# A depthwise convolution re-cut from four 32-channel groups to eight 16-channel groups, with its pointwise on four bands and a fixed order of issue

## The chip, the cores and the metric

The kernel runs on one core of a Trainium2 chip. The metric is the device time of one execution in microseconds (us), the median of several runs. "The profile" and "the trace" are one execution taken by the hardware profiler. Engines: PE (matrix multiply; PEld is its weight load), DVE (vector), ACT (activation), POOL (GpSimd), and SP, whose queue issues nearly all DMAs here.

## The reference, cut to what matters

The input x is 16 images of 256 channels and 64 x 64 pixels, float32. Two layers follow each other:

```python
x = x + linear_attention(gn(x))   # layer 0: group norm, rms norm, q/k/v projection, softmax, context, output, rms norm
x = x + experts(gn(x))            # layer 1: the one that the change touches

def experts(x):                   # a router picks 2 of 4 experts for each image
    out = 0
    for i in the two chosen experts:
        h = depthwise_conv_3x3(x, dw_w[i]) + dw_b[i]     # every channel by itself, padding 1
        h = gelu(h)
        out += weight_i * (pw_w[i] @ h + pw_b[i])        # 256 x 256 over the channels
    return out
```

## The kernel before, in words

All 16 images go through one software pipeline. An image has a load-and-statistics stage, a projection stage, an attention stage and an expert stage, each on the time scale of 64 "slots"; stages of four successive images run side by side. A list of events, each a small function with a time in slots, is sorted by time and traced in that order; the scheduler of the language may then move instructions within its dependences. So image b + 2 is projected and image b + 1 attends while image b is in its expert stage. The projection makes four tiles `pq` for each of an image's eight token groups (`project`, L271) and ACT empties them (`evacuate`, L280 and L281). `po` (L340), `pss` (L257), `pc` (L287), `ptq` (L310) and `tr` (L366) are the other products of layer 0. Seven of the eight PSUM banks form one pool called `bank`.

The expert stage takes an image in four quarters of 16 rows (16 slots each). Its 256 channels are in two halves.

- Channels 128 to 255 go through DVE: `pad1` (L581 to L592) makes a padded copy on ACT, `start1` (L613) and eight `tap1` (L620) accumulate the nine taps for each of the two experts in `acc`, and `gelu1` (L627) finishes.
- Channels 0 to 127 go through PE. `pad0` (L546 to L563) normalizes a quarter into one buffer `pd0`, even and odd rows apart; there is a single `pd0`. `spread` (L569) copies it by DMA: for each of four groups of 32 channels, four DMAs put four row-shifted views on the four quarters of the partitions of a tile `xr`, so that a contraction over 128 partitions is one over 32 channels and 4 rows. That is 16 DMAs a quarter, each of 32 partitions by 528 floats. `conv0` (L598) makes 3 contractions of 512 columns for each group, one for each column offset, whose weights `taps` hold both experts and both row phases on the output partitions. `gelu0` (L605) writes the activated result back into `xr`.
- The pointwise for each half m of the output channels is `pointwise` parts 0 and 1 (L638, `acc`, 128 rows of weights, one bank for each row phase o) and parts 2 and 3 (L645, `xr`, where each row phase uses its own 64 partitions, a tile of 64 rows of the array). Its weights `psp` are spread once an image by 16 DMAs of 32 partitions (`spread_pw`, L529). `residual` (L653) adds the result to the ring of images in SBUF and `store` (L659) writes it out.

The loads are `load_a` (L201, `xa`), `load_b` (L204, `xb`) and `load_x1` (L80, `ring`), two or one DMA for each token group, all on SP's queue, as are `spread`, `spread_pw` and `store`. Every engine and every queue works in order.

The lines of `spread`, as an example of what one quarter issues:

```python
for r in range(NR):                      # NR = 4; called for g = 0..3
    nc.sync.dma_start(out=t[r * CH : (r + 1) * CH],
                      in_=pd0[g * CH : (g + 1) * CH, PH[r] : PH[r] + QF])
```

Of the kernel before, what the change touches and what calls it, by code (L numbers as in the profile page):

```python
# [16 lines left out]
P = 128  # L17
# [23 lines left out]
NR = 4  # L41
CH = P // NR
# [3 lines left out]
QF = QA * PW  # L46
# [3 lines left out]
LOGIT_CAP = 60.0  # L50


@with_exitstack
def pipelined_path(ctx, tc, wqkv, x, w_outT, b_out, g_out, router_wT, router_b, dw, dw_b, pwT, pw_b, out):
# [65 lines left out]

    id32 = const.tile([P, CH], FP, name="id32")
    nc.vector.tensor_tensor(id32, ident[:, 0:CH], ident[:, CH : 2 * CH], ALU.add)
    for r in range(2, NR):
        nc.vector.tensor_tensor(id32, id32, ident[:, r * CH : (r + 1) * CH], ALU.add)

    imask = const.tile([P, TOPK], FP, name="imask")
    nc.gpsimd.memset(imask, 0.0)
    for q in range(NR):
        nc.gpsimd.memset(imask[q * CH : (q + 1) * CH, q % 2 : q % 2 + 1], 1.0)
# [25 lines left out]
    tab = const.tile([P, CGR, NE, 2, 3], FP, name="tab")  # L155
    nc.gpsimd.memset(tab, 0.0)
    btab = const.tile([P, CGR, NE], FP, name="btab")
    for r in range(NR):
        rs = slice(r * CH, (r + 1) * CH)
        for o in range(2):  # L160
            if 0 <= r - o <= 2:
                for g in range(CGR):
                    nc.scalar.dma_start(
                        out=tab[rs, g, :, o, :],
                        in_=dw[g * CH : (g + 1) * CH, :, 3 * (r - o) : 3 * (r - o) + 3],
                    )
        nc.scalar.dma_start(
            out=btab[rs], in_=dw_b[0:P].rearrange("(g c) e u -> c g (e u)", c=CH)
        )


    pd0 = const.tile([P, 2 * (QF + PW)], FP, name="pd0")
    nc.gpsimd.memset(pd0, 0.0)
    PH = [QF + PW, 0, QF + 2 * PW, PW]
# [312 lines left out]
    def pick_rows(b, i):  # L487

        oh = live["oh", b]
        wv = live["wv", b] if i else new(small, [P, CGR, 3, 2, TOPK], "wv", b, bufs=1)  # L490
        wt = new(small, [P, CGR, 6, NE], "wt", b, i, bufs=1)
        nc.vector.tensor_tensor(
            wt, tab.rearrange("p g e o x -> p g (o x) e"),
            oh[:, i].unsqueeze(1).unsqueeze(1).to_broadcast([P, CGR, 6, NE]), ALU.mult,
        )
        nc.vector.tensor_reduce(
            wv[:, :, :, :, i].rearrange("p g x o -> p g o x"),
            wt.rearrange("p g (o x) e -> p g o x e", o=2), AX.X, ALU.add,
        )
# [12 lines left out]
    def build_taps(b, g):  # L512

        wv = live["wv", b]
        t = new(work, [P, 3 * P], f"taps{g}", b, bufs=1)
        nc.gpsimd.tensor_tensor(
            t.rearrange("p (n c) -> p n c", c=CH),
            wv[:, g].rearrange("p x o i -> p (x o i)").unsqueeze(2).to_broadcast([P, 12, CH]),
            id32.unsqueeze(1).to_broadcast([P, 12, CH]), ALU.mult,
        )  # L520

    def spread_pw(b):

        t, src = new(work, [P, CGR, C], "psp", b, bufs=1), live.pop(("pw0", b))
        for o in range(2):
            for i in range(TOPK):
                q = 2 * o + i
                for g in range(CGR):
                    nc.sync.dma_start(  # L529
                        out=t[q * CH : (q + 1) * CH, g], in_=src[g * CH : (g + 1) * CH, i]  # L530
                    )
# [8 lines left out]
    def pad0(b, j, s):  # L540

        sck, bik = scale1(b, 0)
        if s == 0:
            top = pd0[:, QF + PW + 1 : QF + PW + 1 + W]
            if j == 0:
                nc.gpsimd.memset(top, 0.0)  # L546
            else:
                last = QF + PW + QF
                nc.gpsimd.tensor_copy(top, pd0[:, last + 1 : last + 1 + W])
        base = 0 if s == 0 else QF + 2 * PW  # L550
        nc.scalar.activation(
            pd0[:, base : base + QF].rearrange("p (a w) -> p a w", w=PW)[:, :, 1 : W + 1],
            x1c(b, j)[:, 0].rearrange("p (a s w) -> p a s w", s=2, w=W)[:, :, s],
            AF.Identity, bias=bik, scale=sck,
        )
        if s == 1:
            low = pd0[:, QF + 1 : QF + 1 + W]
            if j < NQ - 1:
                nc.scalar.activation(
                    low, x1c(b, j + 1)[:, 0, 0:W], AF.Identity, bias=bik, scale=sck  # L560
                )
            else:
                nc.gpsimd.memset(low, 0.0)  # L563

    def spread(b, j, g):

        t = new(work, [P, QF], "xr", b, j, g, bufs=6)
        for r in range(NR):
            nc.sync.dma_start(  # L569
                out=t[r * CH : (r + 1) * CH],  # L570
                in_=pd0[g * CH : (g + 1) * CH, PH[r] : PH[r] + QF],
            )
# [21 lines left out]
    def conv0(b, j, g):  # L594
        po = live["dw", b, j, g] = bank("dw", b, j, g)
        rows3 = live["xr", b, j, g].rearrange("p (a w) -> p a w", w=PW)
        for d in range(3):
            nc.tensor.matmul(  # L598
                po, live[f"taps{g}", b][:, d * P : (d + 1) * P], rows3[:, :, d : d + W],
                start=(d == 0), stop=(d == 2),  # L600
            )

    def gelu0(b, j, g):

        nc.scalar.activation(  # L605
            live["xr", b, j, g][:, 0:GT], live.pop(("dw", b, j, g)), AF.Gelu,
            bias=live["bv", b][:, g : g + 1],
        )
# [20 lines left out]
    def pointwise(b, j, m, part):  # L629

        ms = slice(m * P, (m + 1) * P)
        if part == 0:
            live["ppw", b, j, m] = [bank("pw", b, j, m, o) for o in range(2)]
        po = live["ppw", b, j, m]
        if part < TOPK:
            h = live["acc", b, j, part].rearrange("p (a o) w -> p a o w", o=2)
            for o in range(2):
                nc.tensor.matmul(  # L638
                    po[o], live["pw1", b][:, part, ms], h[:, :, o], start=(part == 0), stop=False
                )  # L640
            return
        for g in range(2 * part - 4, 2 * part - 2):
            for o in range(2):
                half = slice(o * P // 2, (o + 1) * P // 2)
                nc.tensor.matmul(  # L645
                    po[o], live["psp", b][half, g, ms], live["xr", b, j, g][half, 0:GT],
# [3 lines left out]
    def residual(b, j, m, o):  # L650
        po = live["ppw", b, j, m][o]
        xo = x1c(b, j)[:, m].rearrange("p (a o w) -> p a o w", o=2, w=W)[:, :, o]
        nc.vector.scalar_tensor_tensor(  # L653
            xo, po.rearrange("p (a w) -> p a w", w=W),
# [8 lines left out]

    events = []

    def at(t, f, *args):
        events.append((t, len(events), f, args))

    for b in range(NB):
        T = PERIOD * b  # L670
        for g in range(NG):
            t = T + SLOT * g
            if b:
                at(t - 5, load_a, b, g)
            at(t + 3, stats, b, g)
        for i, f in enumerate((gn0_mean, gn0_dev, gn0_scale, gn0_bias)):
            at(T + 60 + i, f, b)
        for g in range(NG):
            t = T + 65 + SLOT * g
            if b:  # L680
                at(t - 6, load_b, b, g)
            at(t, norm, b, g, 0)
            at(t + 1, norm, b, g, 1)
            at(t + 2, add_squares, b, g)
            at(t + 3, sum_squares, b, g)
            at(t + 3.5, token_scale, b, g)
            for c in range(CG):
                at(t + 5 + c // 2, project, b, g, c)
                at(t + 6 + c // 2 - 0.5, evacuate, b, g, c)
            at(t + 8, context, b, g)  # L690
            at(t + 8, q_sum, b, g)
            at(t + 9, q_norm, b, g)
            at(t + 10, q_turn, b, g)
            at(t + 11, q_keep, b, g)
        at(T + 130, mix_a, b)
        at(T + 131, mix_b, b)
        at(T + 132, mix_c, b)
        for g in range(NG):
            t = T + 136 + SLOT * g
            if b:  # L700
                at(t + 2, load_x1, b, g)
            for hf in range(2):
                at(t + hf, attend, b, g, hf)
                at(t + hf + 0.9, out_squares, b, g, hf)
                at(t + hf + 2, out_scale, b, g, hf)
                at(t + hf + 3, out_norm, b, g, hf)
            for k in range(KH):
                at(t + 5, out_turn, b, g, k)
                at(t + 6, out_add, b, g, k)
                at(t + 7 + k, square_sums, b, g, k)  # L710
        R = T + 201
        at(R, gn1_sums, b)
        at(R + 1, gn1_scale, b)
        at(R + 2, router, b)
        at(R + 3, choose, b)
        at(R + 5, pick_taps, b)
        E = T + 217
        at(E - 9, weigh, b)
        at(E - 8, pick_bias, b)
        at(E - 6, pick_row_bias, b)  # L720
        for i in range(TOPK):
            at(E - 7 + i, pick_rows, b, i)
            for e in range(NE):
                at(E - 5 + 2 * i + e / 2, pick_pw, b, 0, i, e)
                at(E + 11 + 2 * i + e / 2, pick_pw, b, 1, i, e)
        for g in range(CGR):
            at(E + 1 + g, build_taps, b, g)
        at(E + 11, spread_pw, b)
        for j in range(NQ):
            t = E + 16 * j  # L730
            at(t - 3, pad1, b, j)
            for i in range(TOPK):
                at(t - 1 + 7 * i, start1, b, j, i)
# [643 lines left out]
```

## Time and profile before

| | |
|---|---|
| median of 3 runs | 3365.88 us (3356.1 to 3371.1) |
| the profiled execution | 3348.74 us, of which the span of the program is 3346.9 us |
| mean granted PE clock | 0.963 |
| PE busy | 3082.2 us (92%) |
| DVE, ACT, POOL busy | 2366.2, 2222.3, 909.2 us |
| DMAs of `xr`, `psp` | 1024 and 256 |
| ACT table loads | 308, of 1283 ns each |

Shares of busy time are means over the span. Groups give the count, the union of the busy time, the mean of one instruction, and the idle time before it with what ended it. A matmul of float32 stands as two records, each with its own weight load, and the recorded length of one is longer than the distance to the next, because they are pipelined; the distances are what add up. DMA-issuing instructions are not counted as busy; the queue's own timeline shows them.

### The profile page before, as it was taken

How to read it: one execution, taken by the hardware profiler on the slowest of the kernel's cores; microseconds unless marked ns; L12 is line 12 of the kernel's file. 1: busy time of each engine (PE TensorE's matmuls, PEld its weight loads, DVE VectorE, ACT ScalarE, POOL GpSimd, SP SyncE). 2: the span in 40 equal slices, each digit the busy share in tenths (PEclk: the TensorE clock that was granted, in tenths of full speed). 3: DMA queues.
4: the chain of work that ended last, by engine and by line, in shares of the span. 5: the costliest groups of instructions: out<-in, count | busy, mean ns of one | idle time of the engine just before them, and what ended most of it. 6: DMA issues, size and time to landing. Idle time of an engine off the chain costs nothing. (4 is left out here: it accounts for less than half of the span.)

```text
span 3346.9 us, 38011 instructions
## 1 busy us (share of the span) xinstructions
PE 3082.2 (92%) x11476; PEld 1716.7 (51%) x11476; DVE 2366.2 (71%) x4076; ACT 2222.3 (66%) x4308; POOL 909.2 (27%) x943
## 2 busy tenths in 40 slices
PE   4888999999999999999999999999999999999988
PEld 2565555554555555555555555555555555554433
DVE  4447677777677676786776776766786776678886
ACT  2577667676776766767676676767777776775432
POOL 2234222232222322223232222323223232222210
PEclk9798999999999999999999999999999999999999
DMA  7422333334334342342434333332232233222322
GB/s 226 153 81 84 117 92 108 120 89 123 96 92 127 102 127 81 104 127 88 129 92 126 91 108 108 92 99 73 88 101 85 87 95 97 75 77 79 106 70 71
DMA packets 189380, 342.06 MB, mean 102 GB/s; under 512 B 36848, under 2 KB 45552, under 8 KB 189168
## 3 DMA queue, kind: packets, MB, share of 16 engines
q1 hardware_dynamic: 182560, 338.16, 33.1%
q10 hardware_dynamic: 6608, 1.39, 0.2%
q8 instruction: 95, 1.56, 0.2%
q14 instruction: 117, 0.96, 0.1%
HBM read 194.72 MB, written 67.11 MB: 78 GB/s over the span
## 5 line engine op out<-in xcount | busy, mean ns | idle before, releaser
L620 DVE SCALAR_TENSOR_TENSOR acc<-pd,ds,acc 128x1024 f32<-128x1024 f32 x1024 | 1326.0, 1320 | 13.8 <-ACT acc L613 6.7
L598 PE MATMUL dw<-xr,taps 128*128 128x512 f32 x1536 | 740.7, 622 | 0.8 <-DVE ring L653 0.8
L271 PE MATMUL pq<-wqkv_n,xg 128*128 128x384 f32 x2048 | 715.0, 503 | 2.2 <-DVE ring L375 2.2
L271 PEld LDWEIGHTS pq<-wqkv_n,xg 128*128 128x128 f32 x2048 | 394.8, 196 | 317.6 <-issue 69.2
L645 PE MATMUL pw<-xr,psp 64*128 64x512 f32 x2048 | 527.2, 633 | 0.0
L638 PE MATMUL pw<-acc,pw 128*128 128x512 f32 x1024 | 487.6, 600 | 20.0 <-ACT acc L627 20.0
L598 PEld LDWEIGHTS dw<-xr,taps 128*128 128x128 f32 x1536 | 289.8, 198 | 284.2 <-issue 275.3
L302 POOL TENSOR_TENSOR e<-e,qs 128x512 f32<-128x512 f32 x128 | 144.7, 1131 | 1007.3 <-DVE qs L298 666.5
L382 ACT ACTIVATE sqj<-ring,nm 128x512 f32<-128x512 f32 x256 | 184.4, 720 | 333.7 <-DVE ring L375 326.6
L186 POOL TENSOR_TENSOR s<-s,mhalf 128x2 f32<-128x2 f32 x256 | 245.0, 957 | 343.0 <-DVE s L185 342.4
L359 DVE TENSOR_TENSOR ob<-po,s 128x512 f32<-128x512 f32 x256 | 176.9, 691 | 198.9 <-POOL s L186 198.9
L247 ACT ACTIVATE sq<-xb,bi,sc 128x512 f32<-128x512 f32 x240 | 183.9, 809 | 176.2 <-PE pss L257 176.0
L280 ACT ACTIVATE e<-pq,r 128x256 f32<-128x256 f32 x512 | 245.3, 479 | 71.0 <-PE pq L271 69.1
L645 PEld LDWEIGHTS pw<-xr,psp 64*128 64x128 f32 x2048 | 182.4, 192 | 208.3 <-issue 205.7
L638 PEld LDWEIGHTS pw<-acc,pw 128*128 128x128 f32 x1024 | 187.6, 193 | 196.9 <-issue 150.0
L297 DVE TENSOR_REDUCE qs<-e 128x16 f32<-128x512 f32 x128 | 87.6, 684 | 262.0 <-ACT e L280 261.4
L340 PE MATMUL po<-mw,qt 128*128 128x256 f32 x1024 | 263.6, 382 | 0.7 <-DVE ring L375 0.3
L340 PEld LDWEIGHTS po<-mw,qt 128*128 128x128 f32 x1024 | 192.2, 190 | 103.4 <-issue 33.5
L375 DVE SCALAR_TENSOR_TENSOR ring<-tr,gout,ring 128x512 f32<-128x512 f32 x256 | 181.6, 745 | 81.4 <-PE tr L366 81.1
L287 PE MATMUL pc<-vr,e 128*128 128x129 f32 x1024 | 156.1, 285 | 86.5 <-ACT vr L281 82.9
L653 DVE SCALAR_TENSOR_TENSOR ring<-pw,bs,ring 128x512 f32<-128x512 f32 x256 | 184.3, 744 | 63.7 <-PE pw L645 63.7
L251 POOL TENSOR_TENSOR sq<-sq 128x512 f32<-128x512 f32 x128 | 203.0, 1586 | 94.2 <-issue 59.4
(138 smaller groups left out, 3754.3 us busy)
## 6 DMA issues: line engine op xcount, KB each, us to landing
xr<-pd SPq DMA_DIRECT2D x1024, 66.0 KB, 2.0
ring<-in_x SPq DMA_DIRECT2D x256, 256.0 KB, 3.2
out<-ring SPq DMA_DIRECT2D x128, 512.0 KB, 2.8
xa<-in_x SPq DMA_DIRECT2D x120, 512.0 KB, 4.2
xb<-in_x SPq DMA_DIRECT2D x120, 512.0 KB, 4.0
psp<-pw SPq DMA_DIRECT2D x256, 32.0 KB, 1.9
pw<-in_pwT ACTq DMA_DIRECT2D x1, 1024.0 KB, 8.4
wqkv_n<-in_w_qkvT SPq DMA_DIRECT2D x1, 384.0 KB, 3.2
```

The source lines that it names most:

```text
L186: nc.gpsimd.tensor_tensor(out_t, out_t, mhalf[:, :n], ALU.pow)
L247: nc.scalar.activation(live["sq", b, g][:, k], xb[:, k], AF.Square, bias=bi, scale=sc)
L251: nc.gpsimd.tensor_tensor(sq[:, 0], sq[:, 0], sq[:, 1], ALU.add)
L271: nc.tensor.matmul(pq, xg[:, k, c * P : (c + 1) * P], wqkv[:, k], start=(k == 0), stop=(k == KH - 1),)
L280: nc.scalar.activation(live["e", b, g][:, c], pq[:, : 2 * HID], AF.Exp, scale=r)
L340: nc.tensor.matmul(po[:, c], qt[:, n * P : (n + 1) * P], live["mw", b], start=True, stop=True)
L382: nc.scalar.activation(junk, x1(b, g)[:, k], AF.Square, bias=live["nm", b][:, k : k + 1], accum_out=live["sm", b][:, 1, k, g : g + 1],)
L598: nc.tensor.matmul(po, live[f"taps{g}", b][:, d * P : (d + 1) * P], rows3[:, :, d : d + W], start=(d == 0), stop=(d == 2),)
L620: nc.vector.scalar_tensor_tensor(acc, pd1[j % 2][:, t // 3 : t // 3 + QR, t % 3 : t % 3 + W], live["ds", b][:, i, t : t + 1], acc, ALU.mul ...
L638: nc.tensor.matmul(po[o], live["pw1", b][:, part, ms], h[:, :, o], start=(part == 0), stop=False)
L645: nc.tensor.matmul(po[o], live["psp", b][half, g, ms], live["xr", b, j, g][half, 0:GT], start=False, stop=(g == CGR - 1),)
L653: nc.vector.scalar_tensor_tensor(xo, po.rearrange("p (a w) -> p a w", w=W), live["bs", b][:, m : m + 1], xo, ALU.add, ALU.add,)
```

## The change

1. Depthwise on PE: channel groups go from four of 32 to eight of 16. Rows and columns are both split by parity (`pd0` now holds four phases), and each of 8 pieces of 16 partitions of `xr` holds one view: 4 row shifts by 2 column phases. A group needs 2 contractions of 256 columns; two groups share a bank. `spread` issues 8 DMAs of 16 partitions by 264 floats for each group, 64 a quarter. `xr` has 12 buffers in place of 6.
2. The output partitions of a contraction are 4 pixel phases by 2 experts by 16 channels, so the pointwise from `xr` runs on four bands of 32 partitions, one bank for each pixel phase; the pointwise from `acc` reads pixel phases with a stride of two. Four banks are held until both halves m have been added. `residual` runs on 256 elements, eight times a quarter. `psp` takes 64 DMAs of 16 partitions an image.
3. `pad0` writes each row phase by two ACTIVATEs, one for each column phase. `gelu0` runs on 256 elements, eight times a quarter.
4. The tables for the taps are made in the setup by DVE in place of 24 small DMAs.
5. The timetable: all times come from a table `WAIT`, and the events are traced under `tc.manual_schedule()`, so that instructions stay in the order of the list.

```diff
-NR = 4
-CH = P // NR
+NPC = 8
+CH = P // NPC
...
-    pd0 = const.tile([P, 2 * (QF + PW)], FP, name="pd0")
+    pd0 = const.tile([P, 2, 2, QA + 1, PC], FP, name="pd0")
...
+        for v in range(NPC):
+            for g in range(CGR):
+                nc.sync.dma_start(
+                    out=t[v * CH : (v + 1) * CH, g], in_=src[g * CH : (g + 1) * CH, v % 2]
+                )
...
+        def put(rows, slot, n, src):
+            for t in range(2):
+                nc.scalar.activation(
+                    pd0[:, rows, t, slot : slot + n, t : t + W // 2],
+                    src.rearrange("p a (c t) -> p a c t", t=2)[:, :, :, t],
+                    AF.Identity, bias=bik, scale=sck,
+                )
...
-        t = new(work, [P, QF], "xr", b, j, g, bufs=6)
-        for r in range(NR):
+        t = new(work, [P, QA * PC], "xr", b, j, g, bufs=12)
+        for v in range(NPC):
+            a = v // 4
             nc.sync.dma_start(
-                out=t[r * CH : (r + 1) * CH],
-                in_=pd0[g * CH : (g + 1) * CH, PH[r] : PH[r] + QF],
+                out=t[v * CH : (v + 1) * CH],
+                in_=pd0[g * CH : (g + 1) * CH, v // 2 % 2, v % 2, a : a + QA].rearrange(
+                    "c a w -> c (a w)"
+                ),
             )
...
-        for d in range(3):
+        for d in range(2):
             nc.tensor.matmul(
-                po, live[f"taps{g}", b][:, d * P : (d + 1) * P], rows3[:, :, d : d + W],
-                start=(d == 0), stop=(d == 2),
+                po, live[f"taps{g}", b][:, d * P : (d + 1) * P], rows3[:, :, d : d + W // 2],
+                start=(d == 0), stop=(d == 1),
             )
...
-        for g in range(2 * part - 4, 2 * part - 2):
-            for o in range(2):
-                half = slice(o * P // 2, (o + 1) * P // 2)
+        for g in range(4 * part - 8, 4 * part - 4):
+            for q in range(4):
+                band = slice(q * P // 4, (q + 1) * P // 4)
                 nc.tensor.matmul(
-                    po[o], live["psp", b][half, g, ms], live["xr", b, j, g][half, 0:GT],
+                    po[q], live["psp", b][band, g, ms], live["xr", b, j, g][band, 0 : GT // 2],
                     start=False, stop=(g == CGR - 1),
                 )
...
+            at(t + WAIT["pad0"], pad0, b, j, 0)
+            at(t + WAIT["pad0"] + 0.01, pad0, b, j, 1)
+            for g in range(CGR):
+                at(t + WAIT["pad0"] + 0.02 + WAIT["spread"] + WAIT["spread_g"] * g, spread, b, j, g)
+            for g in range(0, CGR, 2):
+                u = t + WAIT[f"conv{g // 2}"]
+                at(u, conv0, b, j, g)
+                at(u, conv0, b, j, g + 1)
+                at(u + WAIT["gelu0"], gelu0, b, j, g)
+                at(u + WAIT["gelu0"], gelu0, b, j, g + 1)
+            t += 2 * SLOT - 0.5 + WAIT["gelu1_1"] + WAIT["pointwise"]
...
     events.sort(key=lambda e: e[:2])
-    for _, _, f, args in events:
-        f(*args)
+    with tc.manual_schedule():
+        for _, _, f, args in events:
+            f(*args)
```

With t the slot at which a quarter begins, the new table puts `pad0` at t + 3, `spread` from t + 3.52 to t + 5.27, the four pairs of `conv0` at 11.37 (groups 2, 3), 12.36 (4, 5), 13.2 (0, 1) and 16.9 (6, 7), and the parts of `pointwise` from t + 16.95 on, one slot apart. `spread_pw` stands at 10.84 of an image's first quarter.

## The prediction

> **What bounds the kernel now.** First the page's engine sums and a steady stretch of the stage table (columns: busy time with the number of instructions for PE, PEld, DVE, ACT, POOL, then PE's granted clock, DMA share, GB/s).
>
> ```profile
> PE 3082.2 (92%) x11476; PEld 1716.7 (51%) x11476; DVE 2366.2 (71%) x4076; ACT 2222.3 (66%) x4308; POOL 909.2 (27%) x943
> 1000.00:2600.00 1600.00, 1516.13 (x5714) 842.66 (x5713) 1152.26 (x1993) 1130.92 (x2160) 447.78 (x453) 0.97 0.34 102
> ```
>
> PE works 95% of steady time, DVE 72%, ACT 71%: PE bounds it. SP is in neither line. So second the timelines of SP's queue at two successive images' psp bursts, and its two kinds of DMA (duration min/median/max in ns, first and last start):
>
> ```profile
> 2147.60 10.03 SPq L529 DMA_DIRECT2D psp<-pw  x16
> 2158.04 0.34 SPq L659 DMA_DIRECT2D out<-ring  x1
> ...
> 2345.12 10.04 SPq L529 DMA_DIRECT2D psp<-pw  x16
> 2355.26 0.53 SPq L659 DMA_DIRECT2D out<-ring  x1
> 2355.88 1.82 SPq L569 DMA_DIRECT2D xr<-pd  x3
> ```
> ```profile
> L569 SPq DMA_DIRECT2D xr<-pd x1024: 507/582/1722, 287.1 to 3316.8; - x171
> L529 SPq DMA_DIRECT2D psp<-pw x256: 512/589/1907, 283.2 to 3244.8; - x128
> ```
>
> An image takes 197.5 us here, 202 in the median over the run; a quarter is 50.5. Sixteen SBUF-to-SBUF DMAs take SP 10.03 us: 0.63 each with the gap, and the same for rows of 1 KB (psp) and of 2.1 KB (xr). An issue costs SP time whatever it carries. Today an image has 80 of them and 40 loads and stores of about 0.45: 68 of 202 us. Third, the waits on the single pd0, which show that the next pad stands behind the last spread:
>
> ```profile
> POOL pd L549 <- DMA xr<-pd: 181.3, 46, 17.5
> ACT pd L551 <- DMA xr<-pd: 56.0, 18, 6.8
> ```
>
> Fourth PE's distances, and its weight loads (columns start, length, what):
>
> ```profile
> 1649.86 5.32 PE L271 MATMUL pq<-wqkv_n,xg 128*128 128x384 f32 x16
> 1655.02 1.03 PE L340 MATMUL po<-mw,qt 128*128 128x256 f32 x4
> 1655.89 2.74 PE L598 MATMUL dw<-xr,taps 128*128 128x512 f32 x6
> ```
> ```profile
> 1613.44 0.30 PEld L217 LDWEIGHTS pg<-mv,gmean 128*128 128x128 f32 x2
> 1613.76 0.30 PEld L645 LDWEIGHTS pw<-xr,psp 64*128 64x128 f32 x4
> ```
>
> From start to start: eight pq matmuls of 384 columns 5.16 us (0.645 each), two po of 256 columns 0.87 (0.43 each). One of 512 takes 0.86. In the second fence two loads of 128 rows take 0.30 us and four loads of 64 rows also 0.30: loads of different row bands run side by side.
>
> **The change, part by part.** *PE.* A quarter's conv0 goes from 12 x 0.86 = 10.3 us to 16 x 0.43 = 6.9: 3.4 less, 14 an image. The pointwise from acc stays 6.9 (16 of 256 columns for 8 of 512). From xr, four bands share the array where two do: 64 matmuls x 0.43 / 4 = 6.9, as now. [...] The load row above (four in the time of two) speaks against queueing, so I count 6.9.
>
> *DVE* gets 8 residuals of 256 (0.49, the pw row of L485) for 4 of 512 (0.74): +0.9 us a quarter, and the picks of the tap tables, 256 elements for 96, under 2 an image: 38 of 50 us become 39. *ACT* gets 8 gelus at about 0.48 (the e row, 256 elements) for 4 at 0.68, and 3 more pad instructions (0.45 to 0.6): +2.7 a quarter, while the program's order needs 110 table loads for 308: -198 x 1.283 = -254 us in all, -4.0 a quarter. *POOL* +2 us an image. The setup loses some ACT DMAs; at most 8 us, before the first statistics are ready. All this is off the path while PE or SP sets it. Four of seven banks held may make PE wait on ACT's evacuations: 0 to 1 us a group; it disappears under what follows. So do the longer lists of waits (PE's separate wait instructions go from 996 to 2313 in the program, 17 to 50 ns each, at most 4 us an image) and what the fixed order shifts elsewhere.
>
> *SP.* The program issues 4096 + 1024 such DMAs for 1024 + 256. Rows of 16 partitions aren't in the trace. Bounds for one: below, 0.43, the distance of an xa load (378 ns, 128 partitions, one side in HBM); above, 0.63, since psp and xr agree although one carries twice the other. The shortest xr issue of 1024 is 0.507. I take 0.63: same path (SBUF to SBUF), same 16-fold division, and size has no effect. So one spread is 64 x 0.63 = 40.3 us, psp another 40.3, and SP needs 5 x 40.3 + 40 x 0.48 = 221 us an image, over the 202 it has. SP becomes the bound even if it never waits.
>
> *It waits, too.* There is one pd0, and under the fixed order the next pad on ACT stands behind the evacuations of a projection, which stands on PE behind the pair of conv0 (slot 16.9) that needs the last spread. Queued behind that one DMA wait on PE: that conv0 (16.9), pointwise parts 0 and 1 (16.95, 17.95), the projection (18.1); on ACT gelu0, four evacuations (18.8), pad0 (19.0); on SP the next spread. From the last issue's end: landing 2.0 - 0.6 = 1.4; conv0 pair 4 x 0.43 = 1.7; pointwise 8 x 0.43 = 3.4; projection 8 x 0.645 = 5.2; last evacuation 0.9 (0.479 + 0.373); pad0 4 at about 0.6 + 2 at 0.43 (from 0.804 at 512 and 0.453 at 64 elements), overlapping, 2.8. Sum 15.4 us. SP has 10 loads and stores for it, 4.8 us, and sits idle for the rest. The other pairs of conv0 are not later: from 75% of the burst to its end PE has two pairs, ptq and tr, about 6 of 10 us. Nor are the 12 buffers of xr: groups 4 to 7 wait for the last pointwise of the quarter before, some 27 us after the handoff starts; the spread reaches them after 15.4 + 20.
>
> So a quarter is 40.3 + 15.4 = 55.7 us, and the first, where psp is issued during the handoff, 40.3 + 4.8 + 40.3 = 85.4. An image: 85.4 + 3 x 55.7 = 252.5. The last two images have no projection behind them: handoff 6.9, fewer loads, 225. PE's 44 us a quarter, DVE's 39 and ACT's 34 fit inside.
>
> Sum: first spread at 287 (as now), 14 x 252.5 = 3535, 2 x 225 = 450, and after the last spread 24 (landing 1.4, conv0 1.7, pointwise 14, residual and store 7): 4296, and 2 outside the span. The profiled execution lies 0.5% under the median of the runs; I say **4300**.
>
> An unknown above: idle waits of PE may lower its clock. The slices at the start, where PE is busy 205 of 287 us, have 0.89 granted: 12% of the 10.3 us of PE in a handoff, 48 times, +60 us. [...]
>
> **The rivals.** *Faster: the small issue is cheap.* If 16 partitions cost c, an image's loop is 320c + 3 x 15.4 + 4.8; it is under 202 for c below 0.47. At 0.43 it is 189, and PE with 202 - 14 = 188 is level: 16 x 12 us less, about 3170. For it: an xa load costs 0.43. Against: no xr or psp issue took under 0.507. [...]
>
> *Slower, but the loop is shorter.* If the pad did not wait for the projection, or c is the 0.57 seen behind an idle moment, then 3800 (issue alone: 287 + 14 x 221 + 2 x 205 + 24) to 3980 (64c = 36.5 with the whole handoff).
>
> *Slower by PE.* Cheap issues, but the bands' loads queue at the 0.11 us that the loads of pss stand apart (seven in 0.86): 128 x 0.11 = 14.1 for 6.9 us a quarter, less 3.4 gained: 54 a quarter, about 3570.
>
> That the contraction isn't halved as said is excluded: the program has 16 conv0 matmuls of 256 columns a quarter.
>
> **How the numbers follow.** The full loop (4000 to 4480) 0.66; the shorter loop (3600 to 4000) 0.18; cheap issue, faster, 0.11; PE's loads 0.03; no change 0.02, where c happens to fall at 0.47. No change is within 0.5%, about what a measurement of this kernel tells apart. Slower 0.87, faster 0.11. The range reaches down into the shorter loop, leaving out the cheap issue and the rest: 3700 to 4480.
>
> **What would show it.** Right: xr issues near 0.58 us, 64 in a row over 40 us; psp bursts 250 us apart; PE's share down to about 66%, its longest waits those of dw on the DMA of xr; pads waiting on evacuations or on xr's DMAs; SP's longest wait that of L586 on ACT. Wrong: xr issues under 0.47; or SP late but pads early (the loop is shorter); or loads of psp one after another at 0.11.

## The result, and the profile after

The changed kernel takes 4518.3 us (median of four runs, 4511.96 to 4521.58) where the kernel before takes 3364.5 on the same chip: a ratio of 1.343, with a 95% interval of 1.3395 to 1.3463. The forecast was 4300 with a range up to 4480. The direction and the mechanism held; the time lies 218 us above the forecast and 38 above the range. The profiled execution took 4521.58 us, its span 4519.8.

The engine sums and the same steady stretch of the stage table as before (busy time with instructions for PE, PEld, DVE, ACT, POOL, then PE's granted clock, DMA share, GB/s):

```profile
PE 3275.1 (72%) x19156; PEld 2423.3 (54%) x19156; DVE 2427.6 (54%) x4368; ACT 2092.9 (46%) x4542; POOL 1093.3 (24%) x1002
1000.00:2600.00 1600.00, 1202.51 (x7124) 891.33 (x7123) 889.75 (x1598) 782.06 (x1686) 414.40 (x360) 0.85 0.27 84
```

No engine of this line is full any more: PE fell from 95% to 75% of steady time, and its granted clock from 0.97 to 0.85. The chain that ended last, by engine, has SP's queue on top:

```profile
SPq 42%; PE 37%; DMA 9%; issue 4%; ACT 2%; DVE 2%; POOL 1%; ACTq 0%; DVEq 0%; POOLq 0%
```

The two kinds of DMA, as groups of one tile (duration min/median/max in ns, first and last start), and SP's timeline over a part of an image:

```profile
L586 SPq DMA_DIRECT2D xr<-pd x4096: 507/587/1921, 273.0 to 4491.4; - x196
L545 SPq DMA_DIRECT2D psp<-pw x1024: 507/587/1646, 316.0 to 4353.8; - x171
```
```profile
2102.05 41.89 SPq L586 DMA_DIRECT2D xr<-pd  x64
2143.99 0.58 SPq L223 DMA_DIRECT2D xb<-in_x  x1
2144.61 0.94 SPq L94 DMA_DIRECT2D ring<-in_x  x2
...
2153.93 1.56 SPq L94 DMA_DIRECT2D ring<-in_x  x2
...
2160.66 42.16 SPq L586 DMA_DIRECT2D xr<-pd  x64
...
2205.51 43.81 SPq L545 DMA_DIRECT2D psp<-pw  x64
...
2253.83 41.38 SPq L586 DMA_DIRECT2D xr<-pd  x64
```

An issue of 16 partitions by 264 floats has the median of 587 ns that one of 32 partitions by 528 floats had before (582), so a spread of four times the pieces takes SP 41.9 us here. Between two spreads lie 16.7 us here (2143.94 to 2160.66), 17.3 in the mean over the middle of the run; loads of `xb` and `ring` are issued at the start of that gap, behind the burst. Now the same gap on PE, in order of time (in brackets the idle time before, and what ended it):

```profile
2145.43 1.40 PE L619 MATMUL dw<-xr,taps 128*128 128x256 f32 x4 [3.96 <-DMA xr<-pd]
2146.62 2.76 PE L660 MATMUL pw<-acc,pw 128*128 128x256 f32 x6
2149.96 0.72 PE L660 MATMUL pw<-acc,pw 128*128 128x256 f32 x2 [0.57 <-DVE ring L394]
2151.06 2.08 PE L660 MATMUL pw<-acc,pw 128*128 128x256 f32 x8 [0.39 <-ACT acc L648]
2152.98 5.32 PE L290 MATMUL pq<-wqkv_n,xg 128*128 128x384 f32 x16
...
2159.88 2.01 PE L668 MATMUL pw<-xr,psp 32*128 32x256 f32 x32
2161.82 1.13 PE L359 MATMUL po<-mw,qt 128*128 128x256 f32 x4
```

The order is the predicted one: the pair of `conv0` (its first half has run at 2140.37, so that two of its four matmuls are left), pointwise parts 0 and 1, the projection. But conv0 and pointwise stand there for 7.55 us (2145.43 to 2152.98), where 5.1 was counted: PE waits for DVE and for ACT in between, and ACT and DVE wait for the two loads that SP issued right behind the burst, at 2143.99 and 2144.61:

```profile
2148.07 0.81 ACT L265 ACTIVATE xg<-xb,bi,sc 128x512 f32<-128x512 f32 x1 [7.50 <-DMA xb<-in_x]
...
2149.96 1.05 ACT L648 ACTIVATE acc<-acc 128x1024 f32<-128x1024 f32 x1
```
```profile
2149.15 0.75 DVE L394 SCALAR_TENSOR_TENSOR ring<-tr,gout,ring 128x512 f32<-128x512 f32 x1 [11.38 <-DMA ring<-in_x]
```

PE's clock falls in such gaps too. Two rows of the stage table, each from PE's last wait in the pointwise to the projection, for the same eight records of the pointwise; the first is the gap above, the second the one that begins at 2353.4:

```profile
2151.06:2152.98 1.92, 1.92 (x9) 1.61 (x9) 1.05 (x4) 1.92 (x4) 0.43 (x1) 1.00 1.06 431
2360.41:2363.37 2.96, 2.96 (x8) 2.33 (x9) 2.58 (x5) 2.96 (x7) 1.47 (x3) 0.62 1.02 413
```

Of 33 gaps in the middle of the run, those without psp, 18 last 16.5 to 16.7 us. The other 15 last 17.7 to 20.0, with a clock of 0.50 to 0.68 behind PE's last wait.

In the fence of PE's gap the last rows answer a rival: 32 records of the four-band pointwise, which are 16 matmuls, take 1.94 us (2159.88 to 2161.82), and 16 x 0.43 / 4 is 1.72. Four bands do run side by side.

Who was late is in the waits of the engines and of SP's queue (total us, times, longest):

```profile
DVE ring L394 <- DMA ring<-in_x: 646.2, 63, 21.4
PE dw L619 <- DMA xr<-pd: 625.1, 204, 8.9
ACT xg L265 <- DMA xb<-in_x: 336.2, 54, 8.5
```
```profile
SPq L94 <- DMA out<-ring: 307.5, 100, 7.4
SPq L586 <- ACT pd L562: 291.3, 78, 14.8
```

PE's longest wait is for `xr`, as forecast, and SP's wait for the pad on ACT is there, though as SP's second longest. The waits of ACT for `xb` (336.2 us) and of DVE for the ring's loads (646.2 us) were not. SP's 5746 DMAs start in this trace in the order in which the kernel lists them, and so do the instructions of ACT and DVE in the pipeline: both engines stand before a load that SP issued only behind the burst.

### The profile page after: what moved, and what is told of

Its sections match the earlier page's. It is cut to its first block, busy times and chain, and to the rows that moved or that the text cites. A ratio compares the mean times of both kernels' runs of the same rounds, so it can differ in the third digit from the quotient of the medians.

```text
span 4519.8 us, 60126 instructions
## 1 busy us (share of the span) xinstructions
PE 3275.1 (72%) x19156; PEld 2423.3 (54%) x19156; DVE 2427.6 (54%) x4368; ACT 2092.9 (46%) x4542; POOL 1093.3 (24%) x1002
## 4 chain that ended last, share of the span: by engine, by line
SPq 42%; PE 37%; DMA 9%; issue 4%; ACT 2%; DVE 2%; POOL 1%; ACTq 0%; DVEq 0%; POOLq 0%
SPq L586 30%; SPq L545 11%; PE pq L290 9%; PE pw L668 8%; PE pw L660 8%; PE dw L619 4%; PE po L359 3%; DMA out<-ring 3%; DMA xb<-in_x 2%; DMA xr<-pd 2%; DMA ring<-in_x 1%; PE pc L306 1%; PE pss L276 1%; PE tr L385 1%; ACT xg L265 1%
## 5 line engine op out<-in xcount | busy, mean ns | idle before, releaser
L619 PE MATMUL dw<-xr,taps 128*128 128x256 f32 x2048 | 728.4, 507 | 676.9 <-DMA xr<-pd 625.1
L619 PEld LDWEIGHTS dw<-xr,taps 128*128 128x128 f32 x2048 | 487.1, 254 | 850.5 <-issue 574.4
L668 PE MATMUL pw<-xr,psp 32*128 32x256 f32 x8192 | 601.4, 410 | 384.9 <-DMA psp<-pw 384.9
L668 PEld LDWEIGHTS pw<-xr,psp 32*128 32x128 f32 x8192 | 441.0, 197 | 490.3 <-DMA psp<-pw 416.2
L660 PE MATMUL pw<-acc,pw 128*128 128x256 f32 x2048 | 589.5, 438 | 72.8 <-DVE ring L394 32.3
L394 DVE SCALAR_TENSOR_TENSOR ring<-tr,gout,ring 128x512 f32<-128x512 f32 x256 | 190.9, 747 | 782.2 <-DMA ring<-in_x 646.2
L660 PEld LDWEIGHTS pw<-acc,pw 128*128 128x128 f32 x2048 | 426.6, 215 | 209.6 <-DVE ring L394 47.2
L627 ACT ACTIVATE xr<-dw,bv 128x256 f32<-128x256 f32 x512 | 213.1, 467 | 665.9 <-PE dw L619 506.8
L367 ACT ACTIVATE junk<-po 128x256 f32<-128x256 f32 x512 | 195.2, 381 | 651.7 <-PE po L359 642.4
L205 POOL TENSOR_TENSOR r<-r,mhalf 128x4 f32<-128x4 f32 x128 | 222.5, 1738 | 882.5 <-DVE r L204 788.7
L265 ACT ACTIVATE xg<-xb,bi,sc 128x512 f32<-128x512 f32 x240 | 193.9, 808 | 339.0 <-DMA xb<-in_x 336.2
L204 DVE TENSOR_SCALAR s<-ss 128x2 f32<-128x2 f32 x256 | 58.1, 227 | 493.4 <-ACT junk L367 493.3
L677 DVE SCALAR_TENSOR_TENSOR ring<-pw,bs,ring 128x256 f32<-128x256 f32 x512 | 222.7, 475 | 46.0 <-PE pw L668 46.0
## 6 DMA issues: line engine op xcount, KB each, us to landing
xr<-pd SPq DMA_DIRECT2D x4096, 16.5 KB, 1.8
```

Source lines behind the costliest of these rows:

```text
L205: nc.gpsimd.tensor_tensor(out_t, out_t, mhalf[:, :n], ALU.pow)
L265: nc.scalar.activation(live["xg", b, g][:, k], xb[:, k], AF.Identity, bias=bi, scale=sc)
L619: nc.tensor.matmul(po, live[f"taps{g}", b][:, d * P : (d + 1) * P], rows3[:, :, d : d + W // 2], start=(d == 0), stop=(d == 1),)
L660: nc.tensor.matmul(po[q], live["pw1", b][:, part, ms], h[:, :, q // 2, :, q % 2], start=(part == 0), stop=False,)
L668: nc.tensor.matmul(po[q], live["psp", b][band, g, ms], live["xr", b, j, g][band, 0 : GT // 2], start=False, stop=(g == CGR - 1),)
L677: nc.vector.scalar_tensor_tensor(xo, po.rearrange("p (a c) -> p a c", c=W // 2), live["bs", b][:, m : m + 1], xo, ALU.add, ALU.add,)
```

## The experiments

Two questions: is it SP's issues and the handoff through the single `pd0` at all (theory A), or PE (B) or the fixed order (C)? And what made each quarter about 4 us longer than forecast? All but the spread through HBM are single runs.

**The pad 1.25 slots earlier.**

```diff
-    "pad0": 3, "spread": 0.5,
+    "pad0": 1.75, "spread": 0.5,
```

> The changed kernel with pad0 at slot 1.75 of its quarter in place of 3, so that on ACT it stands behind gelu0 of the last pair of conv0 but ahead of the four evacuations of the projection. Theory A (SP's queue sets the time: 64 issues of about 0.65 us a quarter, then a handoff of 17 us through the single pd0): the handoff loses the projection and the evacuations, 5 to 6 us in each of 42 handoffs, about 4290 us in all, and spreads start about 11 us after the one before. Theory B (PE sets it: the four-band pointwise and its low clock) and theory C (the fixed order itself costs): no change, 4500 to 4540.

Measured 4312.9 us. The gap between spreads fell to 12 to 14 us (mostly 12.0 to 12.6), the bursts stayed at 41.9, and an image went from 270 to 255 us. SP's wait for the pad fell with it:

```profile
SPq L586 <- ACT pd L562: 74.7, 62, 12.3
```

PE's work is the same, and 205 us went with one entry of the table. The handoff lies on the path; B alone has no place for this.

**The kernel before, with each DMA of its spreads cut in four.** It makes 64 issues a quarter and 64 for `psp`, for the same bytes and the same matmuls as before.

```diff
...
-            nc.sync.dma_start(
-                out=t[r * CH : (r + 1) * CH],
-                in_=pd0[g * CH : (g + 1) * CH, PH[r] : PH[r] + QF],
-            )
+            for h in range(2):
+                for f in range(2):
+                    cs, fs = slice(h * 16, h * 16 + 16), slice(f * QF // 2, (f + 1) * QF // 2)
+                    nc.sync.dma_start(
+                        out=t[r * CH : (r + 1) * CH][cs, fs],
+                        in_=pd0[g * CH : (g + 1) * CH, PH[r] : PH[r] + QF][cs, fs],
+                    )
```

> The kernel before, with each DMA of spread and of the pointwise weights cut into four of 16 partitions and half the columns: 64 a quarter and 64 an image, as in the changed kernel, and nothing else changed. Theory A: SP alone makes most of the loss: 231 us of issues an image, plus up to 4 x 10 for the handoff of the single pd0: 4000 to 4450. Theories B and C: the kernel before's time, 3365 within 1%.

Measured 4148.4 us, beside 3348.9 for the kernel before: 800 us for the number of issues alone. Its issues of 16 partitions have the same length:

```profile
L576 SPq DMA_DIRECT2D xr<-pd x4096: 507/587/2027, 285.9 to 4117.9; - x196
```

**The spread through HBM.** The changed kernel's contraction, bands and timetable stay. One DMA writes `pd0` to a scratch tensor in HBM, and 16 DMAs read it back, each 16 partitions by four groups in one view of the tensor: 17 issues a quarter in place of 64. `psp` likewise takes 9 in place of 64.

```diff
+            via = dram.tile([P, 2, 2, QA + 1, PC], FP, tag="pdd", name=f"pdd_{b}_{j}")
+            nc.sync.dma_start(out=via, in_=pd0)
...
-                in_=pd0[g * CH : (g + 1) * CH, v // 2 % 2, v % 2, a : a + QA].rearrange(
-                    "c a w -> c (a w)"
+                in_=via[g * CH : (g + 4) * CH, v // 2 % 2, v % 2, a : a + QA].rearrange(
+                    "(g c) a w -> c g (a w)", c=CH
                 ),
```

> The changed kernel with its contraction and timetable, but the spread goes through HBM: one DMA writes pd0, 16 DMAs of 16 partitions by 4 groups read it back (17 issues a quarter for 64), and the pointwise weights take 9 an image for 64. Theory A: PE is the bound again, at 50.5 - 3.4 us a quarter plus waits: 188 to 197 us an image, 3130 to 3290 in all, faster than both. Theory B: PE stays slow, over 4200. Theory C: over 4000.

Measured 3016.3 us (median of four, 3014.6 to 3019.5), a ratio to the kernel before of 0.902 with a 95% interval of 0.8975 to 0.9055. It beats both kernels, and by more than was expected. Its engine sums, and a quarter on SP's queue:

```profile
PE 2823.7 (94%) x19156; PEld 2193.2 (73%) x19156; DVE 2433.9 (81%) x4368; ACT 2083.4 (69%) x4542; POOL 1115.4 (37%) x1002
```
```profile
2092.68 0.33 SPq L594 DMA_DIRECT2D pdd<-pd  x1
2095.66 10.87 SPq L598 DMA_DIRECT2D xr<-pdd  x16
...
2135.52 0.33 SPq L594 DMA_DIRECT2D pdd<-pd  x1
```

PE is full again, at a mean granted clock of 0.983, with 2824 us of work where before had 3082 at 0.963; some 60 of these 258 us are clock (an estimate: 3082 x 0.963 / 0.983 is 3019). So the contraction does bring PE about what it says (224 us was forecast for conv0 alone: 14 an image; its busy time fell from 740.7 to 493.3 us), with the four bands and with the fixed order. What cost 1500 us was the way the copies were issued, with the handoff that hung on it.

**The kernel before under the fixed order, and the changed one without it.** The edits put `with tc.manual_schedule():` around the loop over the events in the one, and take it away in the other.

> The kernel before with its own timetable, but the instructions kept in the order of the list (the one part of the change that moves instructions without changing any). Theory A: a few per cent either way, 3250 to 3480, since SP has 80 small issues an image as before. Theory C (the fixed order itself costs): 4000 or more.

> The changed kernel without the fixed order: the scheduler of the language may move instructions. Theory A: SP's 231 us of issues an image stay, so at least 3900; if it also moves pads ahead of the evacuations, nearer 4200 than 4500. Theory C: 3200 to 3400.

Measured 3423.8 us (before 3350.4 on the same chip, single runs) and 4452.1 us. The order moves 2% in the one and 1.5% in the other: C is out. With the scheduler free, the loads go between the 64 issues and the gaps shrink to 10, 2, 2 to 3 and (with psp) 43 us, but a burst then takes longer: 52.7, 59.8 and 60.2 us for the three between 2038.47 and 2214.97.

**PE kept busy.** Thirteen matmuls of 384 columns a quarter, whose result nobody reads, stand ahead of three pairs of `conv0`, where PE otherwise waits for `xr`.

```diff
     def conv0(b, j, g):
+        idle = {6: 6, 0: 5, 4: 2}.get(g, 0)
+        if idle:
+            junk = bank("idle", b, j, g)[:, : 3 * HID]
+            for i in range(idle):
+                nc.tensor.matmul(junk, ones, wqkv[:, 0], start=True, stop=True)
```

> The changed kernel with 13 added matmuls of 384 columns a quarter (8.4 us), whose result nobody reads, put ahead of the pairs of conv0 at which PE waits for DMAs: 2 ahead of groups 4 and 5, 5 ahead of groups 0 and 1, 6 ahead of groups 6 and 7. They fill idle time, so that the granted clock stays up. Theory A: 1.5 us less in each of 48 handoffs, 4430 to 4470, at a clock of about 0.9. Theory B: the low clock is the loss; with the clock back the time falls below 4200.

A miss: 4540.3 us. The mean clock rose from 0.841 to 0.888, and the time did not fall. PE's timeline in a handoff, whose burst ended at 2144.58:

```profile
2142.87 4.04 PE L618 MATMUL idle<-wqkv_n,ones 128*128 128x384 f32 x12
2146.75 1.89 PE L624 MATMUL dw<-xr,taps 128*128 128x256 f32 x8
2148.47 1.06 PE L665 MATMUL pw<-acc,pw 128*128 128x256 f32 x4
2151.01 2.98 PE L665 MATMUL pw<-acc,pw 128*128 128x256 f32 x12 [1.47 <-DVE ring L394]
2153.83 2.42 PE L290 MATMUL pq<-wqkv_n,xg 128*128 128x384 f32 x7
```

At full clock (1.00 in this window) conv0 and pointwise still take 7.1 us (2146.75 to 2153.83), because PE stands 1.47 us before a bank that DVE has not emptied. DVE's L394 in turn waits for the ring's load. So in this gap a late load, not the clock, holds PE. What the clock costs is not settled by this run, because the added matmuls stand on the path themselves: here the last pair of conv0 begins 2.2 us after the burst's end, with both its halves behind them. In 19 of 33 such gaps PE has no wait for a late load at all, and in 14 of these conv0 begins only 3.8 to 5.6 us after the burst's end.

**The loads on another queue.** `load_a`, `load_b` and `load_x1` are issued on POOL's queue.

```diff
-            nc.sync.dma_start(out=x1(b, g)[:, k], in_=cols(x, b, g)[:, k])
+            nc.gpsimd.dma_start(out=x1(b, g)[:, k], in_=cols(x, b, g)[:, k])
...
-        nc.sync.dma_start(out=new(work, [P, KH, GT], "xb", b, g), in_=cols(x, b, g))
+        nc.gpsimd.dma_start(out=new(work, [P, KH, GT], "xb", b, g), in_=cols(x, b, g))
```

> The loads of xa, xb and ring are issued on POOL's queue, so none stands behind a burst of 64 on SP. Theory 1 (the handoff is 17.3 us and not 15.4 because gelu1 and the residuals wait for loads that were queued behind the burst): ACT's waits on xb (336 us) and DVE's on the ring's loads (646 us) fall to under a third, conv0 and pointwise in the handoff take 5 to 6 us for 7.55, the gap between bursts falls by 1.5 to 2.5 us, 42 times, and the time is 4400 to 4455 us. Theory 2 (PE's low clock in the handoff makes the difference): gap as before, 4500 to 4530. Theory 3 (POOL is a worse place: it computes too, and its order puts loads behind its waits): gaps longer, over 4530.

Measured 4403.6 us. The waits of ACT for `xb` and of DVE for the ring's load are gone from the list of waits, and PE's handoff runs through. Two of them, and their rows of the stage table:

```profile
1704.31 1.10 PE L619 MATMUL dw<-xr,taps 128*128 128x256 f32 x4 [2.37 <-DMA xr<-pd]
1705.24 3.79 PE L660 MATMUL pw<-acc,pw 128*128 128x256 f32 x16
1708.87 5.32 PE L290 MATMUL pq<-wqkv_n,xg 128*128 128x384 f32 x16
...
2228.49 1.74 PE L619 MATMUL dw<-xr,taps 128*128 128x256 f32 x4 [3.47 <-DMA xr<-pd]
2230.02 4.82 PE L660 MATMUL pw<-acc,pw 128*128 128x256 f32 x16
2234.68 5.32 PE L290 MATMUL pq<-wqkv_n,xg 128*128 128x384 f32 x16
```

```profile
1704.31:1708.87 4.56, 4.56 (x21) 3.84 (x22) 3.36 (x5) 4.54 (x10) 1.76 (x3) 1.00 0.70 261
2228.49:2234.68 6.19, 6.19 (x20) 5.00 (x21) 2.37 (x4) 4.12 (x8) 1.26 (x3) 0.72 0.52 189
```

The gap between spreads is 15.4 us in the mean (18 gaps of the middle of the run; 17.3 in the changed kernel), and an image takes 262. So the late loads had cost the handoff 2 us. What is left still depends on the clock: in 8 of 33 gaps it is 1.00 over conv0 and pointwise, and they last 13.6 to 14.2 us; in the others it is 0.59 to 0.76, and they last 15.0 to 16.7.

**Two `pd0`.** They alternate, and pad and spread stand eight slots earlier, so that the next pad need not wait for the last spread. (The space for it comes from `qt`, `mw` and a table of the setup.)

```diff
-    "pad0": 3, "spread": 0.5,
+    "pad0": -5, "spread": 0.5,
...
+    pd0s = [const.tile([P, 2, 2, QA + 1, PC], FP, name=f"pd0_{i}") for i in range(2)]
...
+        pd0, before = pd0s[j % 2], pd0s[(j + 1) % 2]
```

> The changed kernel with two buffers pd0, used in turn, and each pad 8 slots earlier; three other buffers are cut to make room (qt 9 to 8, mw 2 to 1, a setup table). Theory A: SP no longer waits for a pad, an image is 4 x 41.8 + 43.4 + 40 x 0.5 = 231 us of issues, 14 of them and two shorter ones from 270 on: about 3950. Theories B and C: no change.

A miss, and the largest: 4977.7 us, slower than the changed kernel. An image takes 304 us; gaps of 15 to 18 us are still there, and three of four bursts are 51 to 54 us long. SP's waits say what took the pad's place:

```profile
SPq L686 <- DVE ring L680: 520.3, 81, 19.5
SPq L589 <- PE pw L671: 484.8, 52, 12.9
...
SPq L589 <- ACT pd L564: 44.6, 37, 20.3
```

The pad (44.6) is out of the way as wanted. But SP takes the list in order: with the spreads eight slots earlier, a store of the quarter before stands ahead of the next spread and waits for its residual, and the `xr` of groups 4 to 7 wait for buffers that the pointwise still reads. If the stores are the cause, they need only leave that queue:

```diff
     def store(b, j, m):
-        nc.sync.dma_start(
+        nc.gpsimd.dma_start(
```

> The version with two pd0 and early spreads, which took 4978 us, with its stores on POOL's queue. Theory 1 (that version was slow because a store of the quarter before stood in SP's queue ahead of the next spread and waited for its residual): the 520 us of store waits on SP go, an image of 304 us loses 25 to 32 us, and the time is 4450 to 4650; the waits of xr for a free buffer (485 us) stay. Theory 2 (the free buffers of xr alone hold the spread, and the stores only wait in their shadow): those waits grow by what the stores lose, and the time stays at 4900 to 5000. If neither held, and the single pd0 were all, it would come to 3950.

Measured 4897.9 us: in time on the second theory's side, but not by its mechanism, as the waits of `xr` for free buffers hardly grow (501 for 485 us). The store waits are gone, and SP waits as long for the pads instead:

```profile
SPq L589 <- ACT pd L564: 504.3, 72, 21.2
SPq L589 <- PE pw L671: 501.4, 49, 14.3
```
```profile
2185.78 0.81 ACT L266 ACTIVATE xg<-xb,bi,sc 128x512 f32<-128x512 f32 x1 [35.14 <-DMA xb<-in_x]
...
2194.94 2.76 ACT L564 ACTIVATE pd<-ring,bi,sc 128x256 f32<-128x256 f32 x6
```

The second fence is ACT's timeline in one gap. ACT stood for 35 us before a load of `xb` that SP issued at 2181.68, right behind a burst, and the pad is queued on ACT behind what that load feeds. So the loop closes a second time, through the loads, and two `pd0` do not open it. Then both must leave the queue:

> Two pd0 and early spreads, with the stores and the loads of xa, xb and ring on POOL's queue; SP issues xr and psp alone. Theory 1 (with two pd0 the handoff came back because the loads stood behind the burst in SP's queue: load, normalization, projection, evacuation, pad, next burst): the 504 us of SP's waits on pads and the 1557 us of ACT's waits on xb go to under a quarter, bursts follow each other in under 6 us, only the free buffers of xr still hold them (6 to 11 us a burst), and the time is 3950 to 4450 us. Theory 2 (the pads are late for another reason): gaps of 15 us stay, 4700 to 4900.

Measured 3886.0 us (the kernel before 3352.8 on the same chip), 64 less than the first theory's range. SP's timeline no longer has gaps, and its wait for the pads is one of 250 us before the first spread and next to nothing after:

```profile
2124.76 41.52 SPq L546 DMA_DIRECT2D psp<-pw  x64
2166.39 154.06 SPq L589 DMA_DIRECT2D xr<-pd  x213
```
```profile
SPq L589 <- ACT pd L564: 254.1, 9, 250.5
SPq L589 <- PE pw L671: 198.2, 50, 9.7
```

An image takes 227.5 us: five bursts of about 41.5 and in each spread a few us of waits for free buffers (a spread is 45.8 in the median). This is the version without any handoff, and 320 issues still cost more than the 202 us of the kernel before.

## Why the prediction came out as it did

**The count of issues: right. Their price: too low by 4%.** 0.63 us was taken; inside a burst two issues stand 0.632 us apart in the median. But 119 of the 5120 last over 0.9 us, up to 1.9, so the bursts are 41.8 us, not 40.3, and psp's 43.3: +6 and +3 us an image, about half of what the image was off. The trace of before had such issues at the same rate (31 of 1280; a longest one of 1722 ns stands in the row that the prediction shows). The prediction took 10.03 us, the shortest of the 16 psp bursts of before; the mean of those after the first is 10.44, which gives 41.8 for 64.

**The handoff: right in its order, mis-sized in its parts.** For the gap at 2143.9 landing is 1.5 us (1.4 counted), projection 5.2 (5.2), the rest to the next spread 2.5 (3.7). The step that failed is conv0 and pointwise, 1.7 + 3.4 counted and 7.55 measured. The sentence behind it is "SP has 10 loads and stores for it, 4.8 us": it counted what the loads cost SP, not that ACT and DVE wait for them once they stand behind 40 us of issues. In the changed kernel the handoff is 17.3 us for 15.4, three times an image: +6 us. Behind psp it is 7.2 where 4.8 was counted: +2. With the loads on another queue it is 15.4 in the mean, the forecast's number, but that is luck. At a clock of 1.00 it is 13.6, since two terms were too high: conv0 takes 0.9 us for the half of the pair that stands behind the landing, not 1.7, and the rest was counted 1.2 too long. The low clock, which the sum left out, fills that up.

**The sum.** 6 + 3 + 6 + 2 is +17 us an image by these medians and means, half of it the price of an issue and half the handoff, and the first 14 images measured 268.7 us in the mean against 252.5: 14 x 16.2 = +227 in all. The first spread came at 273, not 287 (-14), the two last images took 7 us more than 450, and the tail 28 for 24. Together +224 on 4296: 4520, the profiled span.

**The range.** Its upper end, 180 us above the point, carried one unknown, PE's clock. The prediction works +60 of that out from the slices at the start; no run shows the other 120. The unknown itself is real in the rows: a clock of 0.85 in steady time and 0.66 in the stretch where SP issues psp (2205.5 to 2249.4). Behind the last wait of one handoff it is 0.62, but 1.00 in another, and what the longer gaps cost is less than either figure: 17.4 us in the mean of the 33 gaps less the 16.6 of the short ones is 0.8, some 35 us in 42 handoffs (an estimate). The range had nothing for a late load, and nothing for a longer burst.

**The rivals.** *Cheap issues* fell: no xr issue is under 0.507. *PE's loads one after another* fell: 1.94 us for 32 records of the bands. *The shorter loop* did not occur in the changed kernel, but it is what the version with two `pd0` and a queue of its own for the copies runs in: 3886, inside its 3800 to 3980. *DVE, ACT, POOL off the path* held for their busy time (54, 46 and 24%), not for when they get their data. *The fixed order* was rightly put at little: 2% or less.

## What to carry to other kernels

Before a contraction is re-cut over more and smaller partition groups, count the DMAs that the re-cut needs and multiply by the distance between two issues in the trace: here four times as many issues of the same 0.63 us turned a saving of some 14 us of PE an image into an image 67 us longer, and a detour through HBM with a quarter of the issues turned it into a gain of 10%. Loads that stand on the queue of a long burst come late by it (behind bursts of 41.8 us ACT waited up to 8.5 us for `xb` here, and DVE up to 21.4 us for the ring), and who waits for them belongs to the sum of the path, not only their own issue time. A second buffer opens a loop only if no other item of the same queue closes it again: two `pd0` took 4977.7 us with the loads and stores on SP's queue, and 3886.0 us with both on another.

## What the runs showed of the hardware that was not expected

- The length of an SBUF-to-SBUF issue on SP's queue did not depend on what it carries: medians of 582 and 587 ns for 32 partitions by 2.1 KB and for 16 partitions by 1 KB. The issues `xr<-pdd`, with one side in HBM, were shorter although they carry four groups: 424 ns in the median.
- About one issue in 43 of the changed kernel took over 0.9 us, up to 1.9, and one in 41 of the kernel before. The profile page counts 160 packets on the instruction queue q8, for 95 before, and the trace shows the two together: 112 of the 119 long issues of the changed kernel begin between 0.2 us before and 0.5 us after the start of such a packet, and of all 5120 issues only 126 do. Whether the packet makes the issue long was not tested. Why a psp burst takes 43.3 us in the changed kernel and 41.1 with the loads on POOL's queue was not either.
- A higher mean clock (0.888 for 0.841) bought no time where the matmuls that kept it up stood on the path. Where no load was late, the length of a handoff followed the clock: 13.6 to 14.2 us at 1.00, 15.0 to 16.7 at 0.59 to 0.76.
